# A LoRA projection and paged attention in one kernel: rotary angles ahead of the row tables, small loads after GpSimd's constants, and the first scores ahead of the second query rotation

## The chip, the cores and the metric

One NeuronCore of a Trainium2 chip runs the whole kernel in one launch. The metric is device time in microseconds (us) of one execution. The engines are named as the profile names them: PE is TensorE (matmuls and transposes through an identity matrix), PEld its weight loads, DVE is VectorE, ACT is ScalarE, POOL is GpSimd, SP is SyncE, which here only issues DMAs. ACTq, SPq and POOLq are the instruction queues of these engines, from which DMAs are issued.

## What is computed

Everything is float32. There are 8 sequences of 128 tokens and a width of 512. First each sequence gets a LoRA-like product with a 512x512 matrix that its adapter number picks, and adds it:

```
w = weight[adapter_ids]                         # (8, 512, 512)
x = x + einsum('bsi,boi->bso', x, w)
```

Then an attention layer is added, with 32 query heads and 8 key/value heads of size 128. Queries and keys are normalised per head, weighted, and rotated by an angle that grows with position (rotary embedding). Each sequence attends to up to 512 cached keys, which lie in pages of 32 that a block table lists, and to its own 128 new keys:

```
q, k = rope(rmsnorm(x @ Wq.T, qw), pos), rope(rmsnorm(x @ Wk.T, kw), pos)
v = x @ Wv.T
k_all = concat(k_cache[block_table], k);  v_all = concat(v_cache[block_table], v)
probs = softmax(where(valid, q @ k_all.T / sqrt(128), -1e30))
x = x + (probs @ v_all) @ Wo.T
```

`pos = cache_seqlens + arange(128)`, the angles are `pos * inv_freq`, and a cached key is valid when its number is below the sequence's length.

## The kernel before

The main loop has 32 steps: 4 groups of heads (`g`), and in each group the 8 sequences (`b`). One step is 8 query heads, in two halves of 4 (`n` or `j` is 0 or 1) that share one key/value head each. In each step a loop over the 8 heads (L989) issues, for head `h`: the scores on PE (`sc`, L1000), the mask and the row extreme on DVE (L1010, tile `p`), then everything that waits in the list `pending`, the exponential on ACT (L1026), the transposition on DVE of the head before (`tp`, L828), a share of a list of matmul pieces (`main`), the reciprocal on DVE (L1067) and the normalisation on POOL (L1074). The pieces are the next step's projections (`pj_kv`, `pj_q`), the values of the step before (`o`) and its output projection (`out`), all by the helper `group` (L516). The program is written in the order in which each engine is to run it (`manual_schedule`, L97): no scheduler moves an instruction, so the order of the Python calls is the order on each engine's queue, and an instruction that waits holds back all that stand after it on its engine. Extra transposes are put at given heads by the table `turns_at`, filled by `at(i, s, ...)` (L249 to L265): step `i`, head `s`.

PE transposes write to PSUM through a pool of four tiles (`ps_mm`, L94); a fifth tile waits until one of the four has been read. Evictions from PSUM are copies, on ACT (`on_act`) or on DVE (`on_vec`), L882.

The change is all in the prologue, which stands between L882 and the loop at L950, and in step 0. In the order of the program before it does this:

- **Loads.** ACT and SP issue the large loads: x of sequence 0, the adapter matrix of sequence 0 (`raw_lora`, L166), the weights of head group 0 (`raw_kv`, `raw_q`), then x and the adapter matrix of sequence 1, x of sequence 2 and the output weights (L165 to L179). POOL builds the identity (L183), then issues five small loads, each copied to all 128 partitions: the block table `bt_i` (L186), the lengths `len_i` (L191), the inverse frequencies `ivf` (L193) and the two norm weights `wn` (L195, L196). After them it builds its constants with iotas and memsets (L198 to L224).
- **Sequence 0's LoRA product.** Transposes of x and of the adapter matrix (`lw`), then `y` by `lora_y(0)` (L898), which is added to x on DVE (L541, `acc<-y,acc`), by `flush()` at L902. The sum is transposed (`turn_x1(0)`, L906), and the projections `pj_kv` and `pj_q` start from that.
- **Row tables.** `row_numbers()` (L893) turns the block table into row numbers of the caches: a cast on DVE (L335), ten short POOL operations for the keys (L337 to L340) and four for the values (L343). `row_tables((0,))` (L894) makes the indices of group 0 on DVE (L349, L350). With them `gather_k(0, c)` issues the gathers of sequence 0's keys on POOL (`kc`, L567).
- **Angles.** `rope_angles()` (L897): on DVE the angle of each position and frequency, reduced to the range of the sine (L367 to L390), and on ACT the sine and an absolute value (L391, L393). `rope_cos()` (L903) and `rope_table(n)` (L909, L912) finish the tables `CW` and `SW`.
- **Projections of step 0.** `project(0, "kv")`, `"q0"`, `"q1"`. Each ends by putting its rotation (`rotate`, L596) in `pending`: squares on ACT (L603), three products on DVE (L615, L619), a sum (L636), the scale by two short POOL operations (`norm_scales`, L643, L644), and the scaling on ACT (L649).
- **To the loop.** Between the projections and the loop: the gathers of sequence 0's values (`gather_v(0, c)`, L923, tile `vc`), of sequence 1's keys (L932) and of sequence 2's adapter matrix (L942, tile `lraw`), the other groups' row tables (L933), `run(pending)` (L945), which issues the rotation of `q1`, and the mask of step 0 (L946, operation at L589).

In step 0, head 0 takes its scores, then sequence 1's `lora_y(1)`, its sum on DVE (L541) and the transposes of that sum (`turn_x1(1)`, L959), from which step 1's projections start. `turn_k(1, 0)` (L720) transposes step 1's first new key head, at head 7 of step 0 (L260).

Of the kernel before, what the change touches and what calls it, by code (L numbers as in the profile page):

```python
# [11 lines left out]
FP = mybir.dt.float32  # L12
I32 = mybir.dt.int32
# [5 lines left out]
P = 128  # L19
# [33 lines left out]
def lora_then_paged_attention(  # L53
# [121 lines left out]
    for k in range(2):  # L175
# [9 lines left out]
    bt_i = bt_i.rearrange("p a s -> p (a s)")[:, 0 : 4 * B * LC].rearrange("p (c q) -> p c q", q=4)  # L185
    nc.gpsimd.dma_start(  # L186
        out=bt_i.rearrange("p c q -> p (c q)"),
        in_=block_table.rearrange("b n -> (b n)").partition_broadcast(P),
    )
    len_i = const.tile([P, B], I32, name="len_i")  # L190
    nc.gpsimd.dma_start(out=len_i, in_=seqlens.partition_broadcast(P))  # L191
    ivf = const.tile([P, H2], FP, name="ivf")
    nc.gpsimd.dma_start(out=ivf, in_=inv_freq.partition_broadcast(P))  # L193
    wn = const.tile([P, 2, D], FP, name="wn")
    nc.gpsimd.dma_start(out=wn[:, 1, :], in_=k_norm_w.partition_broadcast(P))  # L195
# [5 lines left out]
    for a in range(4):  # L201
        rows = slice(Q4 * a, Q4 * a + Q4)
        nc.gpsimd.iota(
            inner[rows, :],
            pattern=[[0, 1]],
            base=0,
            channel_multiplier=1,
            allow_small_or_imprecise_dtypes=True,
        )
        nc.gpsimd.memset(quad[rows, :], float(a))  # L210

    key_no = const.tile([P, 4, LC, Q4], FP, name="key_no")
    nc.gpsimd.iota(
# [9 lines left out]
    for m in masks:  # L223
        nc.gpsimd.memset(m[:, :, LC, :], 0.0)  # L224


    lora_ix = const.tile([P, B], I32, name="lora_ix")
    lora_rows = lora_w.rearrange("m (p j) i -> (m p) (j i)", j=4)
# [17 lines left out]
    def at(i, s, early, f, n=4):  # L246
        turns_at.setdefault((i + s // 8, s % 8), []).append((early, n * TR, f))

    for i, (g, b) in enumerate(steps):  # L249
        if i == 0:  # L250
            at(i, 2, False, lambda: turn_q(0, 1))
            at(i, 7, False, lambda: turn_q(1, 0))
            for n, h in enumerate((7, 8, 9, 10)):
                at(i, h, False, lambda n=n: turn_weights(("o1", 0, n)))
        if i == last:
            at(i - 1, 6, False, lambda: turn_q(last, 0))
            at(i, 2, True, lambda: turn_q(last, 1))
# [72 lines left out]

    def row_numbers():

        sel, sk, sv, bt_f = (rows_of[n] for n in ("sel", "sk", "sv", "bt_f"))
        key, step, val = (rows_of[n] for n in ("key", "step", "val"))
# [5 lines left out]
        nc.gpsimd.tensor_scalar(key, key, float(PSIZE * G), sk, ALU.mult, ALU.add)  # L340
        for r in range(4):
            rows = slice(32 * r, 32 * r + 32)
            nc.gpsimd.tensor_scalar(  # L343
                val[rows, :], bt_f[rows, :, r], float(PSIZE * G), sv[rows, :], ALU.mult, ALU.add
            )

    def row_tables(groups):
        for g in groups:
            nc.vector.tensor_scalar(key_ix[:, g, :], rows_of["key"], float(g), None, ALU.add)  # L349
            nc.vector.tensor_scalar(val_ix[:, g, :], rows_of["val"], float(g), None, ALU.add)  # L350

# [14 lines left out]
    def rope_angles():  # L366
# [23 lines left out]
        nc.vector.tensor_scalar(ang, ang, PI_BELOW, -PI_BELOW, ALU.min, ALU.max)  # L390
        nc.scalar.activation(sin, ang, AF.Sin)  # L391

        nc.scalar.activation(cos, ang, AF.Abs)  # L393
        rope["sin"], rope["cos"] = sin, cos

    def rope_cos():
        cos = rope["cos"]
# [318 lines left out]
    def turn_k(i, j, copy=None):  # L716
        s = st[i]
        t = ps_mm.tile([P, HID], FP, tag="mm", name=f"kt_{i}_{j}")
        t = t[:, 0:P].rearrange("d (i a) -> d i a", a=4)
        nc.tensor.transpose(t.rearrange("d i a -> d (i a)"), s.k[:, j, :], ident)  # L720
        (copy or nc.scalar.copy)(s.kT[j][:, :, LC, :].rearrange("d a i -> d i a"), t)  # L721
# [180 lines left out]
    flush()  # L902
    rope_cos()  # L903
    for n in range(2, 4):
        turn_weights(("q0", 0, n), on_act)
    turn_x1(0, on_vec)  # L906
    for n in range(2):
        turn_weights(("q1", 0, n), on_act)
    rope_table(1)  # L909
    for _, f in project(0, "kv"):  # L910
        f()
    rope_table(0)  # L912
# [7 lines left out]
        turn_weights(("q1", 0, n), on_act)  # L920
    run(pending)
    for c in range(LC):
        gather_v(0, c)  # L923
    for _, f in project(0, "q1"):
        f()
    turn_x(1, on_vec)
    for c in range(KC):
        turn_lora(1, c, on_vec if c % 2 else on_act, True)
    turn_q(0, 0, on_act)
    turn_k(0, 0, on_act)  # L930
    for c in range(LC):
        gather_k(1, c)  # L932
    row_tables(range(1, G))  # L933
    nc.vector.scalar_tensor_tensor(
# [4 lines left out]
        op0=ALU.mult,  # L939
        op1=ALU.add,  # L940
    )
    gather_lora(2)  # L942
    for _ in range(3):
        load_next()
    run(pending)  # L945
    make_mask(0)  # L946


    prev = None
    for i, (g, b) in enumerate(steps):  # L950
# [38 lines left out]
        for h in range(8):  # L989
# [159 lines left out]
```

## Time and profile before

| what | value |
|---|---|
| median of three runs | 1210.5 us (1209.48 to 1211.23) |
| the profiled execution's own time | 1208.25 us |
| its span, first to last instruction | 1206.5 us |
| PE busy in the span | 1180.7 us (98%) |
| DVE, ACT, POOL busy | 734.2, 530.0, 672.8 us |
| mean granted TensorE clock | 0.997 |

The page gives the busy time of each engine, the span in 40 slices, the chain of work that ended last, and the groups of instructions by source line. Two things help in reading it. Operands are written `out<-in` with tile names, so `acc<-y,acc` at L541 is the sum of the LoRA product into x. And a line of the timeline gives the start, the duration, the engine, the source line, the operation, its operands and how often it stands there in a row (then the duration is that of the row from its first start to its last end); behind it, in brackets, how long the engine was idle just before and what ended that idle time. One slice of the page is 30.2 us, so the prologue, up to the first scores at 48.89 us, is 1.6 slices: it has to be read in the timeline.

### The profile page before, as it was taken

What the parts mean: (1) busy time and instruction counts of PE and PEld (TensorE: products, weight loads), DVE (VectorE), ACT (ScalarE), POOL (GpSimd) and SP (SyncE); (2) the same over time, 40 slices, a digit from 0 to 9 for tenths busy, and PEclk for the clock granted to TensorE, in tenths of its full rate; (3) what the DMA queues carried; (4) which work ended last, traced back from release to release, by engine and by line L of the source; (5) the groups of instructions that cost most, each with busy time, mean ns of one, the idle gap of its engine ahead of it and who ended that gap; (6) DMA issues with size and microseconds to landing.
All of it is one profiled execution on the core that took longest, in us unless ns stands there. A gap on an engine that the chain in (4) does not pass through costs nothing.

```text
span 1206.5 us, 12952 instructions
## 1 busy us (share of the span) xinstructions
PE 1180.7 (98%) x3408; PEld 578.5 (48%) x3408; DVE 734.2 (61%) x1676; ACT 530.0 (44%) x1645; POOL 672.8 (56%) x779
## 2 busy tenths in 40 slices
PE   5799999999999999999999999999999999999998
PEld 4455554454444444444444444444444444444445
DVE  3566566556567676666656766666557655565651
ACT  3464444444444444444444444444444444444442
POOL 4464556455655556566555565665565556555540
PEclk8999999999999999999999999999999999999999
DMA  8258798786998989888898998888899897777761
GB/s 295 97 181 276 263 305 280 264 280 235 302 301 285 342 296 310 287 297 277 291 298 292 324 334 300 283 292 277 280 315 296 280 312 240 256 247 244 264 224 60
DMA packets 187320, 328.26 MB, mean 272 GB/s; under 512 B 13232, under 2 KB 106160, under 8 KB 178288
## 3 DMA queue, kind: packets, MB, share of 16 engines
q1 hardware_dynamic: 124272, 239.23, 58.9%
q10 hardware_dynamic: 49664, 48.12, 12.3%
q0 software_dynamic: 13312, 40.10, 10.2%
q8 instruction: 27, 0.44, 0.2%
q14 instruction: 45, 0.37, 0.1%
HBM read 195.27 MB, written 132.12 MB: 271 GB/s over the span
## 4 chain that ended last, share of the span: by engine, by line
PE 95%; DMA 2%; POOL 1%; DVE 1%; ACT 1%; issue 0%; SPq 0%; ACTq 0%
PE o L516 23%; PE sc L1000 22%; PE pj_q L516 18%; PE out L516 18%; PE pj_kv L516 9%; PE y L516 2%; DMA w_q<-xw_q 1%; PE lw L431 1%; DMA raw_lora<-in_L_cond_weight_dram 1%; PE kt L720 1%; PE x L431 1%; POOL kc L567 0%; PE wt_q L449 0%; PE wt_o L449 0%; DVE acc L541 0%
## 5 line engine op out<-in xcount | busy, mean ns | idle before, releaser
L1010 DVE CUSTOM_DVE_ANT_0 p<-sc,mask 128x640 f32<-128x640 f32 x256 | 210.9, 824 | 398.5 <-PE sc L1000 398.3
L1026 ACT ACTIVATE p<-p,mn 128x640 f32<-128x640 f32 x256 | 211.7, 827 | 324.3 <-DVE mn L1010 320.6
L1000 PE MATMUL sc<-kT,qT 128*128 128x512 f32 (+1 forms) x1024 | 318.4, 433 | 1.7 <-ACT kT L721 1.7
L1074 POOL TENSOR_SCALAR p<-p,rc 128x640 f32<-128x640 f32 x252 | 202.1, 802 | 188.7 <-DVE rc L1067 186.7
L1000 PEld LDWEIGHTS sc<-kT,qT 128*128 128x128 f32 x1024 | 189.9, 190 | 227.2 <-issue 206.4
L516 PE MATMUL pj_q<-w_q,x1T 128*128 128x512 f32 x512 | 237.0, 593 | 1.4 <-DMA w_q<-xw_q 0.7
L516 PE MATMUL o<-pT,vc 128*128 128x512 f32 x512 | 236.8, 592 | 0.0
L516 PE MATMUL out<-w_o,oT 128*128 128x512 f32 (+1 forms) x528 | 235.0, 580 | 0.9 <-ACT oT L795 0.7
L828 DVE STREAM_TRANSPOSE tp<-p 128x640 f32<-128x640 f32 x252 | 210.9, 837 | 4.3 <-POOL p L1074 4.0
L567 POOL DMA_INDIRECT kc<-in_L_cond_k_cache_dram,key_ix x128 | 130.7, 1021 | 31.4 <-issue 30.6
L567 POOL DMA_INDIRECT vc<-in_L_cond_v_cache_dram,val_ix x128 | 127.8, 999 | 33.1 <-issue 32.9
L649 ACT ACTIVATE q<-q,rs 128x128 f32<-128x128 f32 x256 | 81.9, 390 | 140.6 <-POOL q L636 133.7
L516 PEld LDWEIGHTS out<-w_o,oT 128*128 128x128 f32 x528 | 95.7, 190 | 93.5 <-issue 89.9
L516 PEld LDWEIGHTS pj_q<-w_q,x1T 128*128 128x128 f32 x512 | 92.4, 190 | 93.8 <-issue 90.8
L516 PEld LDWEIGHTS o<-pT,vc 128*128 128x128 f32 x512 | 91.9, 190 | 88.5 <-issue 81.5
L516 PE MATMUL pj_kv<-w_kv,x1T 128*128 128x512 f32 x256 | 116.8, 594 | 0.7 <-ACT x1T L433 0.7
L628 POOL TENSOR_TENSOR k<-sw 128x256 f32<-128x256 f32 x31 | 22.9, 740 | 155.9 <-PE kt L720 131.8
L636 POOL TENSOR_TENSOR q<-q,sw 128x512 f32<-128x512 f32 x59 | 74.7, 1265 | 46.4 <-DVE sw L619 46.4
L603 ACT ACTIVATE sq<-pj_q 128x128 f32<-128x128 f32 x256 | 70.8, 276 | 50.5 <-PE pj_q L516 41.5
L644 POOL TENSOR_TENSOR rs<-ss,mhalf 128x6 f32<-128x6 f32 x64 | 78.0, 1218 | 5.3
L516 PEld LDWEIGHTS pj_kv<-w_kv,x1T 128*128 128x128 f32 x256 | 46.0, 191 | 45.6 <-issue 44.5
L516 PE MATMUL o<-pT,vn 128*128 128x512 f32 x128 | 65.4, 593 | 0.0
(117 smaller groups left out, 875.0 us busy)
## 6 DMA issues: line engine op xcount, KB each, us to landing
xp<-tp SPq DMA_DIRECT2D x63, 1280.0 KB, 5.8
pT<-xp SPq DMA_DIRECT2D x63, 1280.0 KB, 6.8
xk<-tk SPq DMA_DIRECT2D x31, 512.0 KB, 7.8
kT<-xk SPq DMA_DIRECT2D x62, 256.0 KB, 6.5
xq<-tq SPq DMA_DIRECT2D x59, 256.0 KB, 4.6
qT<-xq SPq DMA_DIRECT2D x59, 256.0 KB, 5.5
st_q<-in_L_cond_Wq_dram ACTq DMA_DIRECT2D x24, 256.0 KB, 5.4
xw_q<-tw_q ACTq DMA_DIRECT2D x24, 256.0 KB, 3.6
```

The lines of the kernel that those rows point to most:

```text
L431: nc.tensor.transpose(t[:, j, :], blk, ident)
L516: nc.tensor.matmul(y[0], lhsT=lhsT, rhs=rhs, start=(k == 0), stop=(k == len(pieces) - 1))
L567: nc.gpsimd.indirect_dma_start(out=dst[:, c, :], out_offset=None, in_=src, in_offset=bass.IndirectOffsetOnAxis(ap=rows[:, g, at : at + 1], ...
L603: nc.scalar.activation(sq, t[:, h, :], AF.Square, scale=float(D) ** -0.5, accum_out=ss[:, h : h + 1])
L636: add.tensor_tensor(dst, cw, sw[:, 0:heads, :], ALU.add)
L644: nc.gpsimd.tensor_tensor(rs[:, 0:width], ss[:, 0:width], mhalf[:, 0:width], ALU.pow)
L649: nc.scalar.activation(q, q, AF.Identity, scale=rs[:, h : h + 1])
L828: nc.vector.transpose(u.tp[:, :, r, :], u.p.pop(r).rearrange("q (a k) -> q a k", a=4))
L1000: nc.tensor.matmul(sc[:, lo:hi], lhsT=s.qT[j][:, r, :, :].rearrange("d h q -> d (h q)"), rhs=s.kT[j].rearrange("d a c i -> d (a c i)")[:, ...
L1010: nc.vector.tensor_tensor_reduce(out=p, in0=sc[:, 0:LA], in1=masks[i % 2].rearrange("p a c i -> p (a c i)"), scale=1.0, scalar=3.0e38, op0 ...
L1026: nc.scalar.activation(p, p, AF.Exp, bias=unit.mn[:, one], scale=-1.0, accum_out=unit.sm[:, one])
L1074: nc.gpsimd.tensor_scalar(q, p, unit.rc[:, one], 1.0, ALU.mult, ALU.mult)
```

## The change

Six edits. In the source after the change all lines behind L181 move by up to 12; line numbers below without a mark are those of before.

1. POOL: the iotas `par`, `inner` and the memsets `quad` now come first, then the small loads in the order `len_i`, `ivf`, `bt_i`, then `key_no` and the memsets, then the two `wn` loads.
2. DVE: `rope_angles()` without its two ACT operations now comes ahead of `row_numbers()`. The cast of the block table (before at L335) stands inside it, after the positions. The sine and the absolute value become `rope_sin()`, after the copies of the first two `q0` weight transposes. `rope_cos()` moves behind `turn_x1(0, on_vec)`.
3. The indices of group 0 are made on POOL, by the new `first_table`, keys first; the four value operations and the value indices come after the key gathers.
4. `make_mask(0)` moves from the end of the prologue to between `rope_table(1)` and the `kv` projection.
5. The gathers of sequence 1's keys, the other row tables and `lora_ix` move ahead of `project(0, "q1")`. The gathers of sequence 0's values leave the prologue: two are issued at the end of head 1 and two at the end of head 2 of step 0. The last `run(pending)` before the loop goes, so that the rotation of `q1` is issued in head 0 of step 0, after the first scores' mask on DVE and before the exponential on ACT.
6. `turn_k(1, 0)` moves from head 7 of step 0 to head 6.

```diff
     ident = const.tile([P, P], FP, name="ident")
     make_identity(nc, ident)
-    bt_i = work.tile([P, 4, S], I32, tag="oT0", name="bt_i")
...
-    nc.gpsimd.dma_start(out=len_i, in_=seqlens.partition_broadcast(P))
...
-    nc.gpsimd.dma_start(out=wn[:, 0, :], in_=q_norm_w.partition_broadcast(P))
     par = const.tile([P, 1], I32, name="par")
...
         nc.gpsimd.memset(quad[rows, :], float(a))
+    nc.gpsimd.dma_start(out=len_i, in_=seqlens.partition_broadcast(P))
...
+    nc.gpsimd.dma_start(out=ivf, in_=inv_freq.partition_broadcast(P))
+    bt_i = work.tile([P, 4, S], I32, tag="oT0", name="bt_i")
...
         nc.gpsimd.memset(m[:, :, LC, :], 0.0)
+    nc.gpsimd.dma_start(out=wn[:, 1, :], in_=k_norm_w.partition_broadcast(P))
+    nc.gpsimd.dma_start(out=wn[:, 0, :], in_=q_norm_w.partition_broadcast(P))
...
-            at(i, 6 if i else 7, False, lambda i=i: turn_k(i + 1, 0), 1)
+            at(i, 6, False, lambda i=i: turn_k(i + 1, 0), 1)
...
     def row_numbers():
-        nc.vector.tensor_copy(bt_f, bt_i)
...
         nc.gpsimd.tensor_scalar(key, key, float(PSIZE * G), sk, ALU.mult, ALU.add)
+        first_table(key_ix, "key")
+
+    def row_values():
...
+        first_table(val_ix, "val")
...
+    def first_table(ix, name):
+        nc.gpsimd.tensor_scalar(ix[:, 0, :], rows_of[name], 0.0, 1.0, ALU.add, ALU.mult)
...
         nc.vector.tensor_scalar(pos, len_f, par_f, None, ALU.add)
+        nc.vector.tensor_copy(rows_of["bt_f"], bt_i)
...
+    def rope_sin():
         nc.scalar.activation(sin, ang, AF.Sin)
         nc.scalar.activation(cos, ang, AF.Abs)
...
+    rope_angles()
     row_numbers()
-    row_tables((0,))
     for c in range(LC):
         gather_k(0, c)
-    rope_angles()
+    row_values()
     for _, f in lora_y(0):
         f()
     for n in range(2):
         turn_weights(("q0", 0, n), on_act)
+    rope_sin()
     flush()
-    rope_cos()
     for n in range(2, 4):
         turn_weights(("q0", 0, n), on_act)
     turn_x1(0, on_vec)
+    rope_cos()
     for n in range(2):
         turn_weights(("q1", 0, n), on_act)
     rope_table(1)
+    make_mask(0)
...
     for c in range(LC):
-        gather_v(0, c)
-    for _, f in project(0, "q1"):
-        f()
-    turn_x(1, on_vec)
-    for c in range(KC):
-        turn_lora(1, c, on_vec if c % 2 else on_act, True)
-    turn_q(0, 0, on_act)
-    turn_k(0, 0, on_act)
-    for c in range(LC):
         gather_k(1, c)
     row_tables(range(1, G))
     nc.vector.scalar_tensor_tensor(
         out=lora_ix,
...
+    for _, f in project(0, "q1"):
+        f()
+    turn_x(1, on_vec)
+    for c in range(KC):
+        turn_lora(1, c, on_vec if c % 2 else on_act, True)
     gather_lora(2)
+    turn_q(0, 0, on_act)
+    turn_k(0, 0, on_act)
     for _ in range(3):
         load_next()
-    run(pending)
-    make_mask(0)
...
+                if i == 0 and h in (1, 2):
+                    gather_v(0, 2 * h - 2)
+                    gather_v(0, 2 * h - 1)
```

More of the change, by code (lines that the diff above doesn't have):

```diff
@@ L183, in lora_then_paged_attention @@
     make_identity(nc, ident)
-    bt_i = work.tile([P, 4, S], I32, tag="oT0", name="bt_i")
[L185 to L190, printed above, removed]
-    nc.gpsimd.dma_start(out=len_i, in_=seqlens.partition_broadcast(P))
[L192 to L195, printed above, removed]
-    nc.gpsimd.dma_start(out=wn[:, 0, :], in_=q_norm_w.partition_broadcast(P))
     par = const.tile([P, 1], I32, name="par")
@@ L210, in lora_then_paged_attention @@
         nc.gpsimd.memset(quad[rows, :], float(a))
+    len_i = const.tile([P, B], I32, name="len_i")
+    nc.gpsimd.dma_start(out=len_i, in_=seqlens.partition_broadcast(P))
+    ivf = const.tile([P, H2], FP, name="ivf")
+    nc.gpsimd.dma_start(out=ivf, in_=inv_freq.partition_broadcast(P))
+    bt_i = work.tile([P, 4, S], I32, tag="oT0", name="bt_i")
+    bt_i = bt_i.rearrange("p a s -> p (a s)")[:, 0 : 4 * B * LC].rearrange("p (c q) -> p c q", q=4)
+    nc.gpsimd.dma_start(
+        out=bt_i.rearrange("p c q -> p (c q)"),
+        in_=block_table.rearrange("b n -> (b n)").partition_broadcast(P),
+    )
     key_no = const.tile([P, 4, LC, Q4], FP, name="key_no")
@@ L224, in lora_then_paged_attention @@
         nc.gpsimd.memset(m[:, :, LC, :], 0.0)
+    wn = const.tile([P, 2, D], FP, name="wn")
+    nc.gpsimd.dma_start(out=wn[:, 1, :], in_=k_norm_w.partition_broadcast(P))
+    nc.gpsimd.dma_start(out=wn[:, 0, :], in_=q_norm_w.partition_broadcast(P))
     lora_ix = const.tile([P, B], I32, name="lora_ix")
@@ L331, in row_numbers @@
     def row_numbers():
-        sel, sk, sv, bt_f = (rows_of[n] for n in ("sel", "sk", "sv", "bt_f"))
-        key, step, val = (rows_of[n] for n in ("key", "step", "val"))
-        nc.vector.tensor_copy(bt_f, bt_i)
+        sel, sk, bt_f = (rows_of[n] for n in ("sel", "sk", "bt_f"))
+        key, step = (rows_of[n] for n in ("key", "step"))
         for k in range(3):
@@ L340, in row_numbers @@
         nc.gpsimd.tensor_scalar(key, key, float(PSIZE * G), sk, ALU.mult, ALU.add)
+        first_table(key_ix, "key")
+    def row_values():
+        sv, bt_f, val = (rows_of[n] for n in ("sv", "bt_f", "val"))
         for r in range(4):
@@ L390, in rope_angles @@
         nc.vector.tensor_scalar(ang, ang, PI_BELOW, -PI_BELOW, ALU.min, ALU.max)
+        rope.update(ang=ang, sin=sin, cos=cos)
+    def rope_sin():
+        ang, sin, cos = rope["ang"], rope["sin"], rope["cos"]
         nc.scalar.activation(sin, ang, AF.Sin)
         nc.scalar.activation(cos, ang, AF.Abs)
-        rope["sin"], rope["cos"] = sin, cos
     def rope_cos():
```

## Prediction

> **What bounds the kernel now.** I read the engine lines and slices of the page first, then busy time by stage, then the timelines of PE, DVE and POOL up to 90 us. PE is busy for 1180.7 of 1206.5 us, so the change can only win PE's idle time and slow clock. By stage (columns: PE, PEld, DVE, ACT, POOL busy, granted clock, DMA share, GB/s):
>
> ```profile
> 21.47:26.63 5.16, 0.00 (x0) 0.00 (x1) 4.90 (x8) 1.02 (x2) 3.55 (x4) 0.71 1.03 367
> 26.63:37.53 10.90, 10.90 (x34) 6.50 (x35) 6.97 (x14) 6.05 (x15) 0.73 (x1) 0.82 0.14 50
> 56.00:59.71 3.71, 0.07 (x2) 0.03 (x1) 2.76 (x6) 2.51 (x6) 0.80 (x1) 1.00 0.05 20
> 120.00:1080.00 960.00, 958.50 (x2665) 458.21 (x2664) 608.60 (x1381) 423.93 (x1352) 557.35 (x624) 1.00 0.87 289
> ```
>
> The steady loop has 1.5 us idle in 960: it neither gives anything nor takes back what the prologue wins. Two holes are large, and the change aims at both. PE's timeline names who ended them (brackets):
>
> ```profile
> 16.26 3.90 PE L516 MATMUL y<-wT,x1T 128*128 128x512 f32 x8
> 20.00 1.47 PE L449 MATMUL wt_q<-ident,raw_q 128*128 128x128 f32 x12
> 26.63 1.11 PE L449 MATMUL wt_q<-ident,raw_q 128*128 128x128 f32 x4 [5.16 <-DVE acc L541]
> 59.71 0.63 PE L431 MATMUL x<-ident,acc 128*128 128x128 f32 x4 [3.64 <-DVE rc L1067]
> 85.62 1.35 PE L1000 MATMUL sc<-kT,qT 128*128 128x512 f32 x4 [0.90 <-ACT kT L721]
> ```
>
> The sum `acc<-y,acc` needs only y, done at 20.0. DVE's timeline shows what stands ahead of it:
>
> ```profile
> 14.79 0.69 DVE L433 COPY wT<-lw 128x512 f32<-128x512 f32 x1 [1.21 <-PE lw L431]
> 20.70 0.18 DVE L350 TENSOR_SCALAR val_ix<-pages 128x32 int32<-128x32 f32 x1 [1.30 <-POOL pages L343]
> 21.32 0.69 DVE L378 TENSOR_TENSOR rope_q<-pos,ivf 128x512 f32<-128x512 f32 x1
> 25.49 1.09 DVE L541 TENSOR_TENSOR acc<-y,acc 128x512 f32<-128x512 f32 x1
> 58.53 1.03 DVE L541 TENSOR_TENSOR acc<-y,acc 128x512 f32<-128x512 f32 x1
> ```
>
> DVE waits for POOL's row numbers until 20.70, then computes angles for 4.7 us, and only then adds.
>
> [...] 0.71 in the 5.16 us hole and 0.82 behind it, but 1.00 around the 3.64 us hole. [...] the two k scalings, 0.47 us at 42.41, take 1.49 us when POOL's sum began 40 ns ahead:
>
> ```profile
> 110.83 1.25 POOL L636 TENSOR_TENSOR q<-q,sw 128x512 f32<-128x512 f32 x1
> 110.87 1.49 DVE L652 TENSOR_SCALAR k<-k,rs 128x128 f32<-128x128 f32 x2 [0.37 <-POOL rs L644]
> ```
>
> [...] Traffic was 143 GB/s in 4 to 8 us, while POOL's small loads ran, and 362 in 8 to 12.
>
> **Part A, up to the first scores.** Nothing moves ahead of the DVE copy at 14.79, so DVE's next operation starts at 15.40 as before. Lengths, positions and the cast take it to about 15.95; from the first product to the sum the trace has 25.49 - 21.32 = 4.17 us: the sum could start at 20.1, just as y is done. But ten POOL key operations (15.71 to 19.17 before, beside an idle DVE) now run beside the seven angle operations. Bounds: no lock, 20.1; locks all taken in turn, one POOL operation (0.26) between DVE's, six of them, 20.1 + 1.5 = 21.6. I take the upper bound[...]. The sum then ends at 22.7, the transposes of x (0.44 warm) at 23.2, two weight transposes (0.88) at 24.1, and `pj_kv` starts there instead of at 30.50. ACT no longer decides: two copies from 20.5, sine and absolute value from 21.75, two more copies end at 23.9. The hole is 0.9 us, so PE stays warm; `pj_kv` took 3.59 instead of 3.44. Together 30.50 - 24.1 + 0.15 = 6.55. Without locks ACT's copies set 23.6: 7.05.
>
> Behind that, POOL: with locks six of the ten key operations are done when the angles end at 21.7; four more at 0.35 (0.26 and a gap) end at 23.1, the index (0.3) and an issue gap (0.3) let the gathers start at 23.7 instead of 20.96, and the last, 3.93 later as before, at 27.6. Landing took 5.1 to 5.6 us after issue for these four, while the output weights were still coming in; so 33.2 at worst, less once that queue is empty. `kct` wants them at 30.95 (37.35 - 6.4), but only five of its eight transposes need the last one, and behind them stands 0.5 us of slack (the next transposes end at 38.67, their copy waits for squares on ACT until 39.19). Worst: 33.2 + 0.55 - (30.95 + 0.88) - 0.5 = 1.4. I take 0.05, as the queue is draining by then: **A = 6.5** (5.1 to 7.05). Without locks the last gather is issued at 23.8 and lands in time.
>
> Costed at nothing: the mask (0.48) stands where DVE waits for `pj_kv`; the seven table operations (0.6) fall in the 2.33 us of idle before 45.22; the POOL value operations (1.8) end by 31, ahead of the k sum. Uncovered they would cost just that. The two indices that POOL now makes (0.3 each) replace two of 0.18 on DVE; they are in the sums above. The `wn` loads come 2 us later, at about 5.4 and 6.0, and landed 9.2 after issue, so by 15.2; they are wanted at 24.
>
> **Part B, step 0's second hole**, in times of before. POOL issued nine gathers from 41.12 to 52.28 (1.25 each), then the q1 norm until 54.03; ACT's scaling (54.06 to 55.34) and exponential (55.71), reciprocal, POOL's p until 57.74, DVE's tp, and the sum at 58.53. Now four value gathers are gone: five end at 47.4, and the norm follows the squares (51.0), ending at 52.7. The first mask runs at 50.0 to 50.9 in DVE's 2.23 us of idle; the exponential follows ACT's x copy, 51.6 to 52.6; the rotation ends at 53.1 as before; POOL's p is done at 54.1. The second scores (53.09 to 54.17) release the second mask until 55.05, tp until 55.8, and the sum ends at 56.83 instead of 59.66: PE resumes at 56.87, **B = 2.85**. The value gathers (two of 2.5 us) land in POOL's idle 3.88 and 3.82 us before 64.41 and 69.03; first use of `vc` is at 87.24. If they didn't fit, p and DVE's tp would be late by the excess; what is made of them is wanted at 87.24, and was issued at 77.72 with 6.8 to landing, so 2.7 us of that are free. SP's and ACT's queues keep the order of their DMAs; only POOL's are moved, among themselves and past the q1 norm.
>
> **Part C, turn_k(1, 0).** PE's 0.90 us at 85.62 waits for a kT copy that stands on ACT behind qT and w_o. Earlier by a head, it costs ACT 0.39 there; scores then wait for qT only, until about 84.85: **C = 0.75** (0 to 0.9). Its input is scaled at 80.03, PE is there at 80.8.
>
> **Part D, small loads.** `raw_lora` ends PE's wait at 10.89. `len_i` and `ivf` are issued at about 2.4 and 3.0 instead of 2.22 and 2.77, `bt_i` after instead of before them, `wn` 2 us later. They still collide with `raw_lora`. Unknown cost: a gain of 1 us at most (two of five loads leave its way), a loss of 0.7; **D = 0**.
>
> Sum 6.5 + 2.85 + 0.75 = 10.1. Against the profiled execution: 1208.25 - 10.1 = 1198.15 (span 1196.4). That execution lay 2.25 under the median of the runs, so the median goes from 1210.5 to **1200.4**.
>
> **Rivals.**
> - *B's hole stays*, another wait (tp behind POOL, or ACT's new order) taking its place: 1210.5 - 7.25 = 1203.25. For it: four engines hand over there. Against: every hand-over above is priced from rows. 0.12.
> - *Gathers late*, POOL locked out: A = 5.1, so 1201.8. For: ten POOL operations in DVE's shadow. 0.10.
> - *raw_lora earlier by 1 us or more*: 1199.2. 0.10.
> - *Slower: the cast.* On DVE it now stands ahead of the angles and the sum, and waits for `bt_i`, issued third at about 3.7 instead of first at 1.47 (landed 4.9 later). Each us after 15.7 costs one[...]. It decides from a landing at about 24; at 28 it gives 1210.5 - 10.1 + 12.3 + 2 = 1214.7. Against: the slowest small load landed 9.2 us after issue, which is 13. 0.03.
> - *Won time is not kept*, or the order does not bring it: 1210.5. Against: the loop's 1.5 us idle. 0.03.
> - The forecast: 0.62.
>
> **How the numbers follow.** Own range of the forecast 1198.8 to 1202. Reaching to the first three rivals, with 1 us for the spread of runs: 1197.9 to 1204.2. A measurement of this kernel tells about 0.2% (2.4 us) from no change. Faster: 0.62 + 0.12 + 0.10 + 0.10 = 0.94; same 0.03; slower 0.03.
>
> **What would show it.** After: the sum at L541 near 21.6 and `pj_kv` near 24 (A; at 20.1 and 23.6 the locks were not taken); stretched durations of the angle operations and of POOL's key operations; clock 1.00 from 20 to 32; PE's hole before `turn_x1(1)` near 1 us (B); no 0.9 us before step 1's first scores (C); the first `lw` at 10.9 (D). I am wrong if the cast waits for a DMA, if `kct` waits over 1 us for its gathers, or if a new PE wait over 2 us stands in step 0.

## The result, and the profile after

The changed kernel takes 1198.9 us (median of 4 runs, 1198.71 to 1200.44); the kernel before, run beside it, 1210.87 (4 runs, 1209.48 to 1214.05). The ratio is 0.990, 95% interval 0.9879 to 0.9922: faster by 1.0%, 12.0 us in the medians. The profiled execution took 1198.85 us (span 1197.1), against 1208.25 (1206.5) before: 9.4 less, where the sum forecast 10.1.

PE's timeline after (start, duration, engine, line, operation; in brackets the idle time before it and what ended that). Lines are numbered by the changed kernel: L442 and L444 are the transposes and copies that were L431 and L433, L460 and L461 those of the weights (L449, L450), L527 is `group` (L516), L552 the sum (L541), L1009 the scores (L1000), L1076 the reciprocal (L1067).

```profile
9.67 1.97 PE L442 MATMUL lw<-ident,raw_lora 128*128 128x128 f32 x8 [2.77 <-DMA raw_lora<-in_L_cond_weight_dram]
12.42 1.97 PE L442 MATMUL lw<-ident,raw_lora 128*128 128x128 f32 x8 [0.79 <-DVE wT L444]
15.03 1.94 PE L460 MATMUL wt_kv<-ident,raw_kv 128*128 128x128 f32 x8 [0.64 <-DMA raw_kv<-in_L_cond_Wk_dram]
16.76 4.72 PE L527 MATMUL y<-wT,x1T 128*128 128x512 f32 x8
24.61 0.66 PE L460 MATMUL wt_q<-ident,raw_q 128*128 128x128 f32 x4 [0.48 <-ACT w_q L461]
25.10 3.60 PE L527 MATMUL pj_kv<-w_kv,x1T 128*128 128x512 f32 x8
43.50 1.35 PE L1009 MATMUL sc<-kT,qT 128*128 128x512 f32 x4 [0.84 <-ACT kT L732]
51.59 0.66 PE L442 MATMUL x<-ident,acc 128*128 128x128 f32 x4 [0.91 <-DVE rc L1076]
76.87 1.35 PE L1009 MATMUL sc<-kT,qT 128*128 128x512 f32 x4 [0.24 <-ACT qT L741]
```

The 5.16 us hole before the `q0` transposes is gone (0.48 is left of it), the 3.64 us hole is 0.91, the 0.90 us one 0.24. Two waits are new, both ahead of y: 0.79 us for a DVE copy and 0.64 us for the load of Wk, the key weights. Of before, two lines that the readings need:

```profile
10.89 3.87 PE L431 MATMUL lw<-ident,raw_lora 128*128 128x128 f32 x16 [3.99 <-DMA raw_lora<-in_L_cond_weight_dram]
48.89 1.35 PE L1000 MATMUL sc<-kT,qT 128*128 128x512 f32 x4 [0.85 <-ACT kT L721]
```

From the starts of the scores and of x's transposes (before: 48.89, 59.71, 85.62): A, up to the first scores, 48.89 - 43.50 = 5.39; B, from there to the transposes of sequence 1's x, 10.82 - 8.09 = 2.73; C, from there to step 1's first scores, 25.91 - 25.28 = 0.63. A, B and C make 8.75. The last matmuls of the output start 9.39 earlier (1190.17 instead of 1199.56), so 0.64 lie in the rest of the program, where the work is the same: 0.44 of it are waits of PE for weights in the loop (0.17 and 0.53 before, 0.26 after).

DVE's timeline after:

```profile
15.42 0.22 DVE L379 CAST pages<-bt_i 128x128 f32<-128x128 int32 x1
15.56 0.68 DVE L386 TENSOR_TENSOR rope_q<-pos,ivf 128x512 f32<-128x512 f32 x1
17.20 2.14 DVE L395 SCALAR_TENSOR_TENSOR rope_q<-rope_q,rope_q 128x512 f32<-128x512 f32 x3
19.38 0.43 DVE L398 TENSOR_SCALAR rope_q<-rope_q 128x512 f32<-128x512 f32 x1
21.52 1.14 DVE L552 TENSOR_TENSOR acc<-y,acc 128x512 f32<-128x512 f32 x1 [1.71 <-PE y L527]
```

The angles take what they took before (2.14 us for the three products, 0.43 for the clamp at the end), with POOL busy beside them. They end at 19.8, and then DVE waits 1.71 us for y: y, not DVE, now decides the sum. POOL's timeline shows which of the two took longer for running side by side:

```profile
15.73 0.61 POOL L336 TENSOR_TENSOR pages<-pages 128x32 f32<-128x32 f32 x1 [9.57 <-DVE pages L379]
18.09 0.69 POOL L337 TENSOR_SCALAR pages<-pages,sel 128x32 f32<-128x32 f32 x1
20.38 0.25 POOL L338 TENSOR_TENSOR pages<-pages 128x32 f32<-128x32 f32 x1
21.64 1.09 POOL L578 DMA_INDIRECT kc<-in_L_cond_k_cache_dram,key_ix  x1 [0.29 <-POOL key_ix L357]
```

While DVE's angles run, a POOL operation takes 0.34 to 0.69 us; once they are done, 0.22 to 0.29.

### The profile page after: what moved, and what is told of

The parts are those of the page before. It is cut to its first block, busy times and chain, and to the rows that moved or that the text cites. A ratio compares the mean times of both kernels' runs of the same rounds, so it can differ in the third digit from the quotient of the medians.

```text
span 1197.1 us, 12951 instructions
## 1 busy us (share of the span) xinstructions
PE 1179.7 (99%) x3408; PEld 577.1 (48%) x3408; DVE 733.9 (61%) x1674; ACT 530.0 (44%) x1645; POOL 676.6 (57%) x781
## 3 DMA queue, kind: packets, MB, share of 16 engines
q0 software_dynamic: 13312, 40.10, 10.1%
## 4 chain that ended last, share of the span: by engine, by line
PE 95%; DMA 3%; ACT 1%; DVE 0%; SPq 0%; issue 0%; ACTq 0%; DVEq 0%
PE o L527 23%; PE sc L1009 23%; PE pj_q L527 18%; PE out L527 18%; PE pj_kv L527 9%; PE y L527 2%; DMA w_q<-xw_q 1%; PE lw L442 1%; DMA raw_kv<-in_L_cond_Wk_dram 1%; PE kt L731 1%; PE x L442 1%; DMA ids_i<-in_itok_B_dram 0%; ACT w_q L461 0%; PE qt L740 0%; PE wt_o L460 0%
## 5 line engine op out<-in xcount | busy, mean ns | idle before, releaser
L1009 PE MATMUL sc<-kT,qT 128*128 128x512 f32 (+1 forms) x1024 | 318.4, 433 | 1.1 <-ACT kT L732 0.8
L1009 PEld LDWEIGHTS sc<-kT,qT 128*128 128x128 f32 x1024 | 189.9, 190 | 226.4 <-issue 206.2
L527 PE MATMUL pj_q<-w_q,x1T 128*128 128x512 f32 x512 | 236.9, 593 | 1.0 <-ACT w_q L461 0.7
L527 PE MATMUL o<-pT,vc 128*128 128x512 f32 x512 | 236.9, 592 | 0.0
L527 PE MATMUL out<-w_o,oT 128*128 128x512 f32 (+1 forms) x528 | 234.9, 580 | 0.9 <-ACT oT L806 0.7
L527 PEld LDWEIGHTS out<-w_o,oT 128*128 128x128 f32 x528 | 95.7, 190 | 93.5 <-issue 89.9
L527 PEld LDWEIGHTS pj_q<-w_q,x1T 128*128 128x128 f32 x512 | 92.4, 190 | 93.5 <-issue 90.6
L527 PEld LDWEIGHTS o<-pT,vc 128*128 128x128 f32 x512 | 91.9, 190 | 88.5 <-issue 81.5
L527 PE MATMUL pj_kv<-w_kv,x1T 128*128 128x512 f32 x256 | 116.6, 593 | 0.7 <-ACT x1T L444 0.7
L527 PEld LDWEIGHTS pj_kv<-w_kv,x1T 128*128 128x128 f32 x256 | 45.9, 190 | 45.4 <-issue 44.5
L527 PE MATMUL o<-pT,vn 128*128 128x512 f32 x128 | 65.4, 593 | 0.0
```

What stands on the lines that cost most here:

```text
L527: nc.tensor.matmul(y[0], lhsT=lhsT, rhs=rhs, start=(k == 0), stop=(k == len(pieces) - 1))
L1009: nc.tensor.matmul(sc[:, lo:hi], lhsT=s.qT[j][:, r, :, :].rearrange("d h q -> d (h q)"), rhs=s.kT[j].rearrange("d a c i -> d (a c i)")[:, ...
```

## The experiments

Each is the changed kernel with the edit shown, timed beside the kernel before; its ratio to that is given with the interval. Where an experiment adds or leaves out work, the expectation says which. No experiment undoes the second edit as a whole, the third or the fourth: that the angles' new place closes the first hole is read from the timelines of PE and DVE above, and what each of these three edits adds to it was not measured.

**e1, the first edit undone.**

```diff
+    bt_i = work.tile([P, 4, S], I32, tag="oT0", name="bt_i")
...
+    nc.gpsimd.dma_start(out=len_i, in_=seqlens.partition_broadcast(P))
...
+    nc.gpsimd.dma_start(out=wn[:, 0, :], in_=q_norm_w.partition_broadcast(P))
     par = const.tile([P, 1], I32, name="par")
...
-    nc.gpsimd.dma_start(out=len_i, in_=seqlens.partition_broadcast(P))
...
-    nc.gpsimd.dma_start(out=wn[:, 0, :], in_=q_norm_w.partition_broadcast(P))
```

> The changed kernel with its first edit undone: the five small loads stand ahead of POOL's iotas again, in the old order. Theory (the order of the small loads brought raw_lora early, which opened gaps in front of PE's lw and wt_kv transposes, so that PE came to full clock only at 19.0 us and y took 4.72 us): raw_lora ends PE's wait near 10.9 us, the lw transposes run without a gap, y ends near 20.2 instead of 21.48, pj_kv starts near 24.2 instead of 25.10, first scores near 42.6 instead of 43.50, time 0.9 us below the changed kernel's 1198.9: 1198.0. Rival (when the clock rises is a matter of chance, not of the order of loads): first scores at 43.5 give or take 0.3, time 1198.9. Second rival (the old order is worse, as the loads come in the way of raw_lora): first scores at 44 or later, 1199.5.

1197.65 us, ratio 0.9893 (0.9876 to 0.9910). PE's timeline:

```profile
10.81 3.87 PE L442 MATMUL lw<-ident,raw_lora 128*128 128x128 f32 x16 [3.51 <-DMA raw_lora<-in_L_cond_weight_dram]
16.18 3.62 PE L527 MATMUL y<-wT,x1T 128*128 128x512 f32 x8
23.42 3.60 PE L527 MATMUL pj_kv<-w_kv,x1T 128*128 128x512 f32 x8
41.82 1.35 PE L1009 MATMUL sc<-kT,qT 128*128 128x512 f32 x4 [0.84 <-ACT kT L732]
```

All 16 `lw` transposes run in one piece, and the first scores come 1.68 us earlier than in the changed kernel; the times alone would not tell the two apart, as their intervals overlap. The direction was right, the reason not: in e2, e3 and e4, which keep the new order of loads, the adapter matrix landed late (first `lw` at 10.82, 10.88, 11.17) and the gap inside `lw` was there all the same, 0.78 us each time. So it doesn't come from an early landing. It stands in the program. The 16 transposes fill four `lw` tiles, four each; in the changed kernel the third tile waits for the DVE copy of the second, in e1 and in the kernel before for the ACT copy of x, long done. The pool of four PSUM tiles (`ps_mm`) gave it another tile when the program was built. ACT's copy of x stands behind ACT's first activation, and that waits for a 128x1 memset at the end of POOL's constants (6.04 in the changed kernel, the activation at 6.19). A new theory came from that, tested by e5 and e6.

**e2 and e10, the value gathers back in the prologue** (one kernel, run twice).

```diff
     run(pending)
+    for c in range(LC):
+        gather_v(0, c)
     for c in range(LC):
         gather_k(1, c)
...
-                if i == 0 and h in (1, 2):
-                    gather_v(0, 2 * h - 2)
-                    gather_v(0, 2 * h - 1)
```

> The changed kernel with only the four gathers of sequence 0's values put back into the prologue, ahead of sequence 1's key gathers; the rotation of q1 stays in step 0. Theory (the value gathers on POOL were what made the second hole): 4 x 1.3 = 5.2 us more on POOL ahead of the norm of q1, which then starts near 50 instead of 45.71, so the hole before the transposes of step 1's x grows from 0.91 by 2 to 3 us; time 1201.3. Rival (the removal of the run of pending work ahead of the loop made it): POOL waits for the gathers but the hole grows by under 0.7 us; time under 1199.6.

> The same kernel as in the run with only the value gathers put back, once more. Theory (the 2.09 us wait ahead of step 0's first scores in that run, behind two ACT copies that started late without a wait in the program, is a chance event of that execution): this time the wait is 0.84, the hole 0.92, time 1198.9 give or take 0.7. Rival (gathers being issued on POOL at that moment hold up ACT's copies): the wait is again near 2 us and the time above 1201.

e2: 1202.55 us, ratio 0.9920 (0.9901 to 0.9940); one of its six executions took 7205.2 us and is not in the ratio, and without it the median is 1202.2. e10: 1200.2 us, 0.9915 (0.9901 to 0.9929). PE's timeline of e2, then of e10:

```profile
44.92 1.35 PE L1011 MATMUL sc<-kT,qT 128*128 128x512 f32 x4 [2.09 <-issue]
46.69 4.28 PE L527 MATMUL y<-wT,x1T 128*128 128x512 f32 x6
54.70 0.66 PE L442 MATMUL x<-ident,acc 128*128 128x128 f32 x4 [0.92 <-DVE rc L1078]
```

```profile
44.04 1.35 PE L1011 MATMUL sc<-kT,qT 128*128 128x512 f32 x4 [0.84 <-ACT kT L732]
45.66 2.74 PE L527 MATMUL y<-wT,x1T 128*128 128x512 f32 x6
52.13 0.66 PE L442 MATMUL x<-ident,acc 128*128 128x128 f32 x4 [0.91 <-DVE rc L1078]
```

The hole is 0.92 and 0.91 as after: the gathers alone do not make it, and the theory fell. In e2's execution two ACT copies started late, the wait was 2.09 instead of 0.84, and PE was slower behind it (4.28 instead of 2.74 us for six matmuls of y, at a granted clock of 0.59 in 46 to 48 us and 0.56 in 48 to 50). The repeat has neither. Why ACT was late there stays open, and so does whether it is rare: three of e2's executions took 1202.2 to 1203.1 us, and e10's median is 0.6 above the range expected, though its interval overlaps that of the changed kernel.

**e3, the run of the pending work back ahead of the loop.**

```diff
     for _ in range(3):
         load_next()
+    run(pending)
```

> The changed kernel with only the run of the pending work put back ahead of the loop, so that the rotation of q1 (squares on ACT, products on DVE, norm on POOL) is issued before the first mask on DVE; the value gathers stay in step 0. Theory (the gathers made the hole): the rotation's DVE products (2.0 us) stand ahead of the first mask, which moves from 44.88 to about 46.5, the reciprocal and p with it; the hole grows by 0.5 to 1.5 us, time 1199.8. Rival (the order of the rotation made the hole): the hole grows by 2 us or more, time 1201.3.

1202.08 us, ratio 0.9931 (0.9912 to 0.9950). PE's timeline, and the same stretch by stage (PE, PEld, DVE, ACT, POOL busy, granted clock, DMA share, GB/s):

```profile
53.92 1.09 PE L442 MATMUL x<-ident,acc 128*128 128x128 f32 x4 [2.80 <-DVE rc L1077]
54.80 1.91 PE L460 MATMUL wt_o<-ident,acc 128*128 128x128 f32 x8
```

```profile
51.12:53.92 2.80, 0.00 (x1) 0.03 (x1) 2.50 (x5) 1.88 (x4) 0.80 (x1) 0.96 0.00 0
53.92:57.00 3.08, 3.08 (x13) 2.92 (x14) 0.00 (x0) 1.42 (x3) 2.60 (x3) 0.50 0.08 24
```

The rival held: the rotation's place makes the hole, 1.89 us more of it, and behind it the granted clock was 0.50 (53.92 to 57.00), which cost 1.5 more (26.81 instead of 25.28 us to step 1's first scores). ACT shows how the place works:

```profile
48.27 1.28 ACT L660 ACTIVATE q<-q,rs 128x128 f32<-128x128 f32 x4 [2.21 <-DVE q L647]
```

This scaling of `q1` stands ahead of the first exponential here (49.92); in the changed kernel only the squares of the rotation stand ahead of it, and the scaling (47.83) follows the exponential (45.98).

**e9, both at once.** The edits of e2 and e3 together.

> The changed kernel with both halves of the fifth edit undone: the gathers of sequence 0's values in the prologue, ahead of sequence 1's key gathers, and the run of the pending work ahead of the loop. Theory (the rotation of q1 makes the hole and the gathers only add where POOL's norm stands behind them): the norm starts near 47.5 as in the run with the gathers alone, the scaling of q1 on ACT, and behind it the first exponential, come about 0.6 us later than in the run with the rotation alone; the hole before the transposes of step 1's x is 3.3 to 3.7 us (2.80 with the rotation alone, 3.64 before), time 1202.3. Rival (the gathers cost nothing even then): a hole of 2.8 us. If the clock falls to half behind the hole, 1.5 us more are lost.

1205.38 us, ratio 0.9950 (0.9935 to 0.9965). PE's timeline, ACT's, then the stage:

```profile
56.04 1.09 PE L442 MATMUL x<-ident,acc 128*128 128x128 f32 x4 [3.66 <-DVE rc L1079]
```

```profile
50.38 1.28 ACT L660 ACTIVATE q<-q,rs 128x128 f32<-128x128 f32 x4 [3.06 <-POOL rs L655]
```

```profile
56.04:60.00 3.96, 3.96 (x14) 3.26 (x15) 0.00 (x0) 1.76 (x3) 0.79 (x1) 0.50 0.00 0
```

3.66 us, the 3.64 of before: the gathers add 0.86 where the norm of `q1` on POOL stands behind them, and behind that the scaling and the first exponential on ACT (the scaling waits for POOL here, for DVE in e3). The median is 3 us above the expectation. The profiled execution (1206.37) is 4.1 above it: 2.7 is the clock of 0.50 behind the hole (38.84 instead of 33.37 us between the first scores of the two steps, 2.75 of it hole), and 1.7 a late prologue (first scores at 45.21).

**e4, the cast behind the angles.**

```diff
-        nc.vector.tensor_copy(rows_of["bt_f"], bt_i)
...
         nc.vector.tensor_scalar(ang, ang, PI_BELOW, -PI_BELOW, ALU.min, ALU.max)
+        nc.vector.tensor_copy(rows_of["bt_f"], bt_i)
```

> The changed kernel with the cast of the block table moved behind the angles on DVE, so that POOL's ten key operations run after the angles and not beside them. Theory (POOL paid the whole price of sharing, DVE none, and there is slack behind the gathers): angles on DVE unchanged (three products 2.14 us); POOL's operations fall back to 0.24 to 0.30 us each, start near 20.0 and end near 23.5, first gather near 23.8 and last near 27.7 instead of 25.56; the transposes of the keys wait under 0.8 us; time 1198.9 to 1199.7. Rival of the prediction (late gathers cost the program): the transposes of the keys wait 1.4 us or more, 1200.3 or above. If DVE had been stretched after all, its angle chain gets shorter than 4.2 us and the time falls.

1200.61 us, ratio 0.9927 (0.9908 to 0.9947). The timelines of POOL, DVE (the first product and the end of the angles) and PE:

```profile
21.53 0.24 POOL L336 TENSOR_TENSOR pages<-pages 128x32 f32<-128x32 f32 x1 [15.38 <-DVE pages L398]
22.95 0.30 POOL L337 TENSOR_SCALAR pages<-pages,sel 128x32 f32<-128x32 f32 x1
25.64 1.54 POOL L578 DMA_INDIRECT kc<-in_L_cond_k_cache_dram,key_ix  x1 [0.29 <-POOL key_ix L357]
```

```profile
17.06 0.69 DVE L385 TENSOR_TENSOR rope_q<-pos,ivf 128x512 f32<-128x512 f32 x1
20.89 0.43 DVE L397 TENSOR_SCALAR rope_q<-rope_q 128x512 f32<-128x512 f32 x1
```

```profile
32.68 1.29 PE L722 MATMUL kct<-ident,kc 128*128 128x128 f32 x8
```

Alone, POOL's eleven operations take 3.82 us from first to last; beside the angles they took 5.62. DVE's angles take the same either way (4.26 us alone, 4.25 beside POOL, from the first product to the end). So POOL paid 1.8 us and DVE nothing. The gathers start 4 us later than in the changed kernel, and the key transposes take 1.29 us instead of 1.04: in this execution late gathers cost at most 0.25. It has a span of 0.8 more than the changed kernel's, and 0.7 of that lies in y, which ended at 22.19 instead of 21.48. The median lies 1.7 above. Two of the six executions took 1203.71 and 1204.47 us, at a mean granted clock of 0.996 where the other four have 1.000; what made PE wait or slow down in them, late gathers or something else, was not seen.

**e5, one memset moved.** The zero that ACT's first activation reads stands directly behind the identity; the loads keep the new order.

```diff
     make_identity(nc, ident)
+    rope["one"] = const.tile([P, 1], FP, name="one")
+    nc.gpsimd.memset(rope["one"], 0.0)
     par = const.tile([P, 1], I32, name="par")
...
-    rope["one"] = const.tile([P, 1], FP, name="one")
-    nc.gpsimd.memset(rope["one"], 0.0)
```

> The changed kernel with one memset moved: the 128x1 zero [...] stands directly behind the identity on POOL, ahead of the iotas and of the small loads. The order of the small loads stays as changed. In the program this turns the waits of the adapter's transposes (lw) to copies that are long done: no lw waits for the DVE copy of the lw before last any more. Theory (the first edit's cost is not in its loads; it moved that memset's place in time, the pool handed out its PSUM tiles in another order, and the third lw waits 0.78 us for a copy on DVE, which leaves PE a gap and a late clock): no PE wait inside lw, y takes 3.5 to 3.9 us instead of 4.6 to 4.8, first scores at 41.8 give or take 0.4 if the adapter matrix lands near 10.9, time 1197.6. Rival (the loads' order itself costs): the gap goes but the first scores stay at 43 or later, 1198.9.

1197.42 us, ratio 0.9888 (0.9873 to 0.9902). PE's timeline:

```profile
11.36 3.68 PE L442 MATMUL lw<-ident,raw_lora 128*128 128x128 f32 x16 [4.58 <-DMA raw_lora<-in_L_cond_weight_dram]
15.93 3.66 PE L527 MATMUL y<-wT,x1T 128*128 128x512 f32 x8
23.20 3.60 PE L527 MATMUL pj_kv<-w_kv,x1T 128*128 128x512 f32 x8
41.60 1.35 PE L1009 MATMUL sc<-kT,qT 128*128 128x512 f32 x4 [0.84 <-ACT kT L732]
```

**e6, its counterpart: the old order of loads (the edit of e1) and one iota more ahead of that memset.**

```diff
+    nc.gpsimd.iota(
+        key_no,
...
     mhalf = const.tile([P, GQ + GK], FP, name="mhalf")
```

> The counterpart: the small loads in the old order, ahead of the iotas, as in the run that undid the first edit, plus one iota more on POOL (0.65 us of added work, its output unchanged) ahead of the memset of that 128x1 zero. In the program the third lw then waits for the DVE copy again. Theory (slot order): a PE wait of about 0.78 us ahead of the third lw, y 4.6 to 4.8 us, first scores at 43.5 to 44.3, time 1199.3. Rival (the loads' order): first scores near 41.8 as with the first edit undone, 1197.7.

1200.09 us, ratio 0.9910 (0.9897 to 0.9924). PE's timeline:

```profile
14.41 1.97 PE L449 MATMUL lw<-ident,raw_lora 128*128 128x128 f32 x8 [0.78 <-DVE wT L451]
17.88 3.76 PE L534 MATMUL y<-wT,x1T 128*128 128x512 f32 x8
43.66 1.35 PE L1016 MATMUL sc<-kT,qT 128*128 128x512 f32 x4 [0.84 <-ACT kT L739]
```

The wait goes with the tile that the pool hands out, not with the order of the loads: new order without it, first scores at 41.60; old order with it, 43.66. Counted from the first `lw`, that is 30.24 and 32.00 us. The expectation that y would be slow with the wait failed here (3.76).

**e7, the sixth edit undone.**

```diff
-            at(i, 6, False, lambda i=i: turn_k(i + 1, 0), 1)
+            at(i, 6 if i else 7, False, lambda i=i: turn_k(i + 1, 0), 1)
```

> The changed kernel with the sixth edit undone: the first new key head of step 1 is transposed at head 7 of step 0 again. Theory: step 1's first scores wait 0.90 us for the kT copy instead of 0.24 for qT, the stretch from the transposes of step 1's x to step 1's first scores takes 25.9 instead of 25.28, time 0.65 above the changed kernel: 1199.5. Rival (the kT copy was not what held them): the stretch stays at 25.3, 1198.9.

1199.5 us, ratio 0.9903 (0.9889 to 0.9918). PE's timeline:

```profile
75.91 1.35 PE L1009 MATMUL sc<-kT,qT 128*128 128x512 f32 x4 [0.90 <-ACT kT L732]
```

The 0.90 us wait for kT is back; from the first scores of step 0 to these, 34.03 us instead of 33.37: 0.66. The time alone would not have told it from nothing.

**e8, sine behind the `q0` copies.**

```diff
-    rope_sin()
     flush()
     for n in range(2, 4):
         turn_weights(("q0", 0, n), on_act)
+    rope_sin()
```

> The changed kernel with the sine and the absolute value behind all four copies of the q0 weights on ACT. Theory (after the change ACT, no longer DVE, sets the start of the first projection): the PE wait of 0.48 us for a q0 copy goes, pj_kv starts 3.1 us after the end of y instead of 3.62, the tables CW and SW come 0.5 later on DVE and are hidden behind pj_kv; time 0.5 below the changed kernel: 1198.4. Rival (the DVE copy of x's transpose is as late, or the later tables hold up the rotation): pj_kv starts 3.4 us or more after y, or the wait comes back ahead of the next weights: 1198.9 or above.

1198.59 us, ratio 0.9894 (0.9880 to 0.9908). PE's timeline:

```profile
17.12 3.66 PE L527 MATMUL y<-wT,x1T 128*128 128x512 f32 x8
23.93 3.67 PE L527 MATMUL pj_kv<-w_kv,x1T 128*128 128x512 f32 x8
```

The 0.48 us wait is gone: `pj_kv` starts at 23.93, 3.15 after y's end at 20.78 (3.62 in the changed kernel), and no new wait stands behind it. The time alone would not have told it from nothing.

**e11, PE kept busy in its first waits** (on e5).

```diff
+    busy(8)
     turn_x(0, on_act)
...
     turn_weights(("kv", 0, 3), on_vec)
+    busy(16)
```

> The changed kernel with the memset moved (no slot wait in lw), and PE kept busy while it waits for its first loads: 8 transposes of the identity into a PSUM tile that nothing reads stand ahead of the transposes of x, and 16 more ahead of lw (added work, the output unchanged). Theory (PE's clock[...] is what makes the time from lw to the end of y): lw x16 takes under 2.6 us instead of 3.68 to 3.87 unless the second half of the adapter matrix is late, y takes 3.45 us, the first scores come 1 to 2 us earlier than the 41.6 without the added work, 1196. Rival (the adapter matrix and Wk set the pace, not the clock): y ends within 0.5 us of before, 1197.4; if the added transposes stand in the way, up to 2 us later.

1198.49 us, ratio 0.9902 (0.9887 to 0.9917). PE's timeline:

```profile
11.11 1.10 PE L442 MATMUL lw<-ident,raw_lora 128*128 128x128 f32 x8 [0.74 <-DMA raw_lora<-in_L_cond_weight_dram]
12.55 1.06 PE L442 MATMUL lw<-ident,raw_lora 128*128 128x128 f32 x8 [0.35 <-DMA raw_lora<-in_L_cond_weight_dram]
14.55 1.06 PE L460 MATMUL wt_kv<-ident,raw_kv 128*128 128x128 f32 x8 [0.93 <-DMA raw_kv<-in_L_cond_Wk_dram]
15.45 3.60 PE L527 MATMUL y<-wT,x1T 128*128 128x512 f32 x8
30.40 0.77 PE L722 MATMUL kct<-ident,kc 128*128 128x128 f32 x5 [0.38 <-DMA kc<-in_L_cond_k_cache_dram,key_ix]
```

Eight transposes now take 1.1 instead of 1.97 us, yet y starts only 0.48 earlier than in e5 and the first scores at 41.45 instead of 41.60. What the faster transposes gave went into three waits for the loads of the adapter matrix and Wk, and here the keys' gathers are late too (0.38). The rival held: the loads set the pace.

**e12, e5 and e8 together.**

> Both helpful edits together: the memset moved ahead (no wait inside lw), and the sine and the absolute value behind the four q0 copies on ACT. Theory (they act on different waits): no PE wait inside lw and none for a q0 copy, pj_kv starts 3.1 us after the end of y, first scores at 41.4 or earlier if the adapter matrix lands near 11, time 1197.0. Rival (once the slots are in order, ACT's copies are in time anyway and the sine's place is worth nothing): the same as with the memset alone, 1197.4.

1197.13 us, ratio 0.9887 (0.9870 to 0.9903): the lowest median, though not to be told from e5's or e1's. Neither the `q0` wait nor the DVE wait inside `lw` is there. The adapter matrix landed early (first `lw` at 9.13), its second half and Wk did not (waits of 0.71 and 0.26), y ran slow (4.65), and the first scores came at 42.03.

## Why the prediction was right, and where it was off

The mechanism was right in the main: two holes and a short wait, each smaller by the edit aimed at it, and no new wait of 2 us behind them. What it missed is a new wait ahead of y, which of DVE and POOL would be held up, and the clock behind the second hole. The time, 1198.9, lies in the range, 1.5 under the forecast of 1200.4; that it came so close is in part luck, as two errors of opposite sign met (last point).

- **A was 5.39, not 6.5**, by three terms.
  - *POOL beside DVE*, what the forecast calls locks. I put six POOL operations in turn between DVE's, 1.5 us; that DVE would lose them was my estimate; the trace of before shows one pair in which it is DVE that is held up (two scalings, 1.49 instead of 0.47 us beside a POOL sum). e4 shows 0 on DVE and 1.8 on POOL: beside this back-to-back row of DVE operations it was POOL that was held up each time (0.24 to 0.30 us becomes up to 0.69). What makes an operation longer there was not shown. So the other bound of that term, A = 7.05 with `pj_kv` at 23.6, was the one to take: e1 and e5 reach 7.07 and 7.29. (Their `pj_kv` rows start at 23.42 and 23.20; the forecast counts from the end of the transposes ahead of them, 23.59 and 23.37.)
  - *A new wait ahead of y*, 0.78 or 0.79 us in every kernel with that order of tiles, 0 in e1, e5, e11 and e12. The forecast costed the first edit by the loads' traffic alone and did not compare what each transposition waits for in the two programs. In seven profiles with the wait (e2, e3, e4, e6, e8, e9, e10) y starts 6.22 or 6.23 us after the first `lw`, against 5.37 before and in e1: 0.85. That the order of tiles makes the wait is shown by e5 and e6, which turn it off and on with the loads the other way round; by what rule the pool chose is not seen in a trace.
  - *y itself*. y ended at 21.48 after the change and at 19.80 in e1: 1.68 later, the whole difference between their A (5.39 and 7.07). Of it 1.10 is y's own length (4.72 instead of 3.62) and 0.58 its later start. The first `lw` had come early (9.67, against 10.89 before), but 0.79 for the tile, 0.64 for Wk and 0.29 of slower transposes put y's start 0.50 later than before. y's length varies without a cause that the runs show: with the wait it took 3.66 to 4.83 in nine profiles, without it 3.60 to 4.65 in five, before among them. Whether the wait makes a slow y likelier stays open.
- **B was 2.73, forecast 2.85.** Right in size; e3, e9 and e10 show the shares. The rotation's place in the order is worth 1.89 us; the removal of the gathers, which my text put first, 0.86 in the profiles and only together with it. What the forecast left out is the clock: behind a hole of 2.80 us (e3) and one of 3.66 (e9) the granted clock was 0.50 (53.92 to 57.00 and 56.04 to 60.00), behind one of 3.64 (before) it was 1.00 (59.71 to 65.71), and behind e2's wait of 2.09 us it was 0.59 and 0.56. The length of the hole alone does not part these four, and no limit follows from them; what decides was not shown. In executions in which the clock falls the edit is worth up to 5.5 us (38.84 - 33.37 in e9).
- **C was 0.63, forecast 0.75**; e7, by itself, 0.66. The scores wait for qT now, as the forecast said, 0.24 us.
- **D was put at 0.** The first `lw` came at 9.13 to 12.25 us in the eleven profiles with the new order and at 10.81 to 11.66 in the three with the old one: no effect of the order can be seen, and the rival *raw_lora earlier* came true in the profile after the change (9.67), by chance as far as these profiles show, without bringing anything, since Wk then came late (a wait of 0.64) and y ran slow (4.72). What the edit cost is the new wait ahead of y, under A.
- **The cast** waited for no DMA: 15.42, right behind the DVE copy. The 2 us of slow clock in the sum of that rival were my estimate; in before, 10.90 us at a clock of 0.82 behind the 5.16 us hole come to 1.96. **Gathers late**: e4 delays them by 4 us, and its profile shows a loss of at most 0.25, so the slack there was larger than I priced; in two of its six executions more was lost, by a cause not seen.
- **From the profile to the median** I carried 2.25 us, by which the profile of before lay under its runs. The profile after the change lies at its median, and before's lies 2.6 under the newer median: the medians moved by 12.0, the profiles by 9.4. The granted clock of the runs points to a reason. Beside the experiments the kernel before ran 38 times: 23 at a mean clock of 0.993 or 0.994 (median 1211.7 us) and 15 at 0.995 to 0.997 (1209.4 us). Its profile is one of the better kind (0.997, with a clock of 1.00 behind the 3.64 us hole), and the four runs after the change all have 1.000. My estimate from these means and from e9 is that the clock fell behind that hole in most runs of before, and that closing the hole saved that too; no trace of such a run shows it.
- **The sum.** A, B and C came to 8.75 where I forecast 10.1, 1.35 too much; 0.64 came from the loop, for which I had put nothing. The 2.25 was too large by 2.2. The two errors went against each other, and the second was the larger: 2.2 - 1.35 + 0.64 is the 1.5 by which the forecast was too high.

## What to carry to other kernels

Read which engine decides a hole after the change, not only before it: once DVE was out of the way, ACT's copies (0.48 us, gone in e8) decided, and ahead of y the loads (e11). A pool of buffers makes the order of releases part of the program: compare what each instruction waits for in the two programs, since moving a 128x1 memset, or delaying it, here switched a 0.78 us wait on PE off and on. A hole like these should be priced twice, once with the clock held and once with it lost: a granted clock of 0.50 to 0.59 followed waits of 2.09, 2.80 and 3.66 us here, and 1.00 one of 3.64.

## What was not expected of the hardware

DVE lost nothing to POOL in a row of seven operations, two-input products among them (0.71 us each with and without POOL beside them), while POOL's operations of 0.24 to 0.30 us stretched to as much as 0.69. The other way round occurs too: in the profile of before that the prediction shows, two k scalings on DVE took 1.49 instead of 0.47 us when a POOL sum had begun 40 ns ahead. PE's durations, not the clock column, tell its speed in the first microseconds: eight transposes of `lw` took 1.97 us after the change (from 9.67) and 1.06 in e11 (from 12.55), and the column gives 1.00 for both. The load of the adapter matrix let the first `lw` start at 9.13 to 12.25 us in the eleven profiles with the new order of loads, 3.1 us apart, which is more than most of the edits here are worth; starts relative to that landing are what can be compared.
